# Two transformer layers on one core: the row-maximum steps of layer two's attention take other places among its projections

## The chip, the cores and the metric

The kernel runs on one core of one Trainium2 chip. Time is the device time of one execution in microseconds (us); before the change it is 1713.32 us, the median of three runs (1712.89 to 1716.47). The core's engines run beside each other, each through its own queue of instructions, in the order of that queue: TensorE (PE: matrix products and transposes, results in the accumulation memory PSUM), VectorE (DVE), ScalarE (ACT), GpSimd (POOL), and SyncE (SP), which issues most of the DMAs. An instruction starts when its queue has come to it and when what it waits for on other engines is done.

## The reference, cut to what matters

Two layers work on a sequence of 2048 tokens with 512 features. In each, a branch of attention and a feed-forward branch read the same normalised input, and both are added to the stream. Layer one is linear attention beside a mixture of 16 experts. Layer two, where the change lies, is

```
qkv  = xn @ w_qkv                          # xn: 2048 x 512, w_qkv: 512 x 1536
q, k = rope(rmsnorm(q)), rope(rmsnorm(k))  # per head; 16 heads of 32
s    = q @ k.T / sqrt(32), masked: 0 <= i - j <= 1024
out  = softmax(s) @ v @ w_out
idx  = top 256 tokens by xn . w_router     # these go through a small block of their own
```

The softmax needs the largest score of every row (query and head). This kernel computes the scores twice: once early, only to take the maxima, and once later, transposed, for the probabilities. The change moves pieces of the first of these two passes.

## The kernel before, in words

**Stages.** Layer one fills the span up to about 721 us. From there to 1014 us the loop `for t in range(NT)` (line 959) goes over 16 tiles of 128 tokens and projects each to q, k and v: the stage of the change. From 1014 to 1330 us the 256 chosen tokens pass their own attention and feed-forward block, and from 1330 us to the end come the probabilities and the output of layer two's attention.

**One token tile of the stage.** For `j` = 0, 1, 2 (q, k, v) PE makes four products of 128x128 by 128x512 into one PSUM tile `pj` (pool `ps4`, three buffers); the document calls them Q0..Q3, K0..K3, V0..V3. Each is two matmul records in the trace, at line 965. After q come the four transposes of the next tile's input (`turned`, tile `tr`), after k those of the *previous* tile's finished q, after v those of its k (`turned_qk`, line 776, tile `trqk`). All these transposes, and those of the maxima (`tn`), share one PSUM buffer, pool `ps_t4`; it comes free when ACT or DVE has copied its content out. At the end of a tile `normed_qk` (line 748) is issued: ACT squares q and k out of PSUM (line 754), DVE sums them per head (`rr`, line 755), ACT takes a root, DVE a reciprocal (line 79), two DVE multiplications (line 758) write `qk` and so free q's and k's `pj` buffers, and POOL (DVE for the last tile) applies the rotation (lines 763 to 773).

**The steps.** `maxima(i, ps_a)` (line 616) is a generator. Each of its steps, for one group of four heads and one chunk of keys, makes the scores of 128 queries on PE (line 633: four heads side by side, 32 rows each; eight records), adds masks where the chunk lies at an edge (lines 639, 641), and lets DVE reduce the 128x1024 to 128x2048 scores to maxima (line 645). A step issues no DMA. The scores lie in the tile `pa`, four PSUM banks, with **one** buffer: a step's products wait until the reduction of the step before has read it. After the last step of a query tile come four small reductions (lines 649 to 653), and with the step after that the transposes `tn` and a copy to `negT` on ACT. The 16 query tiles make 144 steps.

**Where steps are written.** `early = Steps(ps_a)` hands them out. `early.some(below)` (line 675) adds 0.9 to a balance and issues a step for each whole one, if one is allowed: query tiles lower than `below` alone, since a tile's q and k must have been transposed. A refused call sets the balance to zero. Before the change there are five calls a tile: after Q1, after q's product and the input transposes, after K1, after k's product and the transposes of q, and after v's product and the transposes of k. From the rate and the limits follow 65 steps: 62 in the loop from the end of tile 1 on, in the later tiles five and four in turn (five in the odd ones), and three written after the loop. The 79 that remain are spread over the next stage at (144 - done) / 182 per unit of work (line 1005).

**The routing.** `routing()` (line 783) finds the 256 tokens by counting: six scans of a 2048-wide row on DVE (line 853, `ge_h` and `ge_l`), each with small PE products (`pc_h`, `pc_l`) in the shared buffer and short work on DVE and POOL, after a row has gone out to DRAM and back by SP's queue; then lists are made on POOL. It is a generator too; `next(route)` is called after the second product of q, k and v, and after each whole product.

**What sets the order.** The loops give a *written* order. The queues do not follow it to the letter: a planner at build time lays the instructions out per engine by its own durations, and puts an instruction whose buffer or input it expects to be missing behind later ones that are ready. So PE's order in the trace is the written order with some steps put off by a few products.

Of the kernel before, what the change touches and what calls it, by code (L numbers as in the profile page):

```python
# [38 lines left out]
def two_layer_kernel(ctx: ExitStack, tc: tile.TileContext, a: dict, out: bass.AP):  # L39
# [29 lines left out]
    def load(eng, dst, src):  # L69
        eng.dma_start(out=dst, in_=src)  # L70
# [45 lines left out]
    def scopy(o, i):  # L116
        S.copy(o, i)  # L117
# [10 lines left out]
    with ExitStack() as l0:  # L128
# [208 lines left out]
        with ExitStack() as p3:  # L337
# [127 lines left out]
            for b in range(NTB):  # L465
# [39 lines left out]
                if b == NTB - 1:  # L505
# [15 lines left out]
                    def turned(t, pool, tag):  # L521

                        xn = xnq.pop(t)
                        if t + 2 < NT:
                            load_xn(t + 2)
                        xnt = xt4.tile([P, NC, P], F32, tag="xnt", name=f"xnt_{t}")
                        transpose4(
                            pool, lambda c: xn[:, c * P : (c + 1) * P], xnt, f"tr2_{t}", scopy, tag
                        )
                        return xnt  # L530
# [11 lines left out]
                for i in range(TB // P):  # L542
                    t = b * (TB // P) + i
                    xr.append(wk.tile([P, D], F32, tag="xr", name=f"xr_{t}", bufs=4))
                    load(nc.sync, xr[i], res_d[t * P : (t + 1) * P, :])
                for i in range(TB // P):
                    t = b * (TB // P) + i
# [172 lines left out]
    early = Steps(ps_a)  # L720


    with p4:
# [24 lines left out]
        def normed_qk(t, pp):  # L748

            qk = wk.tile([P, 2, HEADS, HD], F32, tag="qk", name=f"qk_{t}")  # L750
            t1 = wka.tile([P, 2, HEADS, HD], F32, tag="t1", name=f"t1_{t}")
            rr = wka.tile([P, 2, HEADS], F32, tag="rr", name=f"rr_{t}")
            for j in range(2):
                S.activation(t1[:, j].rearrange("p h d -> p (h d)"), pp[j], AF.Square)
            V.tensor_reduce(rr, t1, AX.X, ALU.add)
            rsqrt_into(rr, rr, eps_h)
            for j in range(2):
                V.tensor_tensor(  # L758
                    qk[:, j], pp[j].rearrange("p (h d) -> p h d", d=HD),
                    rr[:, j].unsqueeze(2).to_broadcast([P, HEADS, HD]), ALU.mult,  # L760
                )
            rope = V if t == NT - 1 else G
            rope.tensor_tensor(
                t1, qk, cosg[:, t].unsqueeze(2).to_broadcast([P, 2, HEADS, HD]), ALU.mult
            )
            t2 = wka.tile([P, 2, HEADS, HD], F32, tag="t2", name=f"t2_{t}")
            for lo, s0 in ((0, HH), (HH, 0)):
                rope.tensor_tensor(
                    t2[:, :, :, lo : lo + HH], qk[:, :, :, s0 : s0 + HH],
                    sing[:, t, :, lo : lo + HH].unsqueeze(2).to_broadcast([P, 2, HEADS, HH]),  # L770
                    ALU.mult,
                )
            rope.tensor_tensor(qk, t1, t2, ALU.add)
            return qk

        def turned_qk(t, qk, j):
            dst, cp = ((qT, scopy), (kT, vcopy))[j]
            transpose4(
                ps_t, lambda g: qk[:, j, 4 * g : 4 * g + 4, :].rearrange("p h d -> p (h d)"),
                dst[:, :, t * P : (t + 1) * P], f"trqk_{t}_{j}", cp,  # L780
            )
# [174 lines left out]
        route, gathering = routing(), []  # L956
        early.place(ps_t, "tr", 0.9)
        last_qk = None
        for t in range(NT):
            pp = []  # L960
            for j in range(3):
                pj = ps.tile([P, D], F32, tag="pj", name=f"p{j}_{t}")
                for c in range(NC):
                    w = w_v[:, c, :] if j == 2 else w_qk[:, c, j * D : (j + 1) * D]
                    PE.matmul(pj, xnt[:, c, :], w, start=c == 0, stop=c == NC - 1)  # L965
                    if c == 1:

                        if j < 2:
                            early.some(t - 1)
                        if t > 0:  # L970
                            next(route, None)
                pp.append(pj)
                if t > 0:
                    next(route, None)
                if j == 0 and t < NT - 1:
                    next_xnt = turned(t + 1, ps_t, "tr")
                    if t + 1 in (NT - 5, NT - 2, NT - 1):
                        gathering.append(t)
                elif j > 0 and last_qk is not None:
                    turned_qk(t - 1, last_qk, j - 1)  # L980
                early.some(t if j == 2 else t - 1)
            xnt = next_xnt
            vt = wk.tile([P, D], F32, tag="vt", name=f"vt_{t}")
            scopy(vt, pp[2])
            load(nc.sync, v_d[t * P : (t + 1) * P, :], vt)
            last_qk = normed_qk(t, pp)
# [517 lines left out]
```

## Time and profile before

| what | value |
|---|---|
| median of three runs | 1713.32 us |
| the profiled execution: its own time / its span | 1715.47 / 1713.8 us |
| PE busy over the span | 1657.4 us (97%) |
| DVE busy over the span | 982.5 us (57%) |
| stage of the change, 721 to 1014 us: PE busy / idle | 268.5 / 24.5 us |
| the same stage: DVE / ACT / POOL busy | 192.6 / 56.8 / 140.9 us |

In the rows of the profile, "busy" sums the time of instructions; "idle before" is the time that an engine waited ahead of a group, with the engine, tile and line that ended the wait. PE is the engine that is nearly always busy, so time is lost where PE waits. PE's weight loads stand as an engine of their own (PEld); they overlap the products, and a wait there is not by itself lost time. The sign `x6` behind a form counts records; two records are one product of 128x512. PEclk is the share of the full clock that PE was granted.

### The profile page before, as it was taken

The page shows a single profiled execution, that of the slowest core. Times are in us where ns is not written, and L with a number is a line of the kernel's source. Part 1 is how long each engine was busy: PE and PEld are TensorE (multiplying, and loading weights), DVE is VectorE, ACT ScalarE, POOL GpSimd, SP SyncE. Part 2 cuts the span into 40 slices and gives each one's busy share as a digit, 9 for nine tenths or more (in the row PEclk, how much of TensorE's full clock was granted, in tenths as well). Part 3 has the DMA queues.
Part 4 walks back from the last instruction along what each step waited for, and adds up shares of the span by engine and source line. Part 5 has one row for each costly group of instructions (what it writes and reads, how often), then busy time and mean ns, then how long its engine had stood idle before and what let it go on. Part 6 is the DMA issues. An engine that isn't in the chain of part 4 may idle for free.

```text
span 1713.8 us, 20410 instructions
## 1 busy us (share of the span) xinstructions
PE 1657.4 (97%) x8114; PEld 743.6 (43%) x8114; DVE 982.5 (57%) x1256; ACT 588.2 (34%) x939; POOL 500.0 (29%) x398
## 2 busy tenths in 40 slices
PE   8999999999999999989999989899999999999999
PEld 3445444444444444444443434454564333333343
DVE  4754746345445543357566676675555477557565
ACT  3213333243253344221111110431100566447473
POOL 3230000000000200053574423330000677558584
PEclk9999999999999999999999999999899999999999
DMA  9411001120030431111010034112232300110101
GB/s 360 169 37 47 25 25 37 47 88 25 25 111 25 94 104 50 62 56 56 25 32 26 28 118 153 62 50 74 74 99 74 99 1 2 50 50 2 50 1 38
DMA packets 62384, 109.23 MB, mean 64 GB/s; under 512 B 12528, under 2 KB 14064, under 8 KB 61520
## 3 DMA queue, kind: packets, MB, share of 16 engines
q1 hardware_dynamic: 55856, 106.12, 18.7%
q0 software_dynamic: 1152, 1.21, 0.4%
q10 hardware_dynamic: 5280, 0.59, 0.3%
q8 instruction: 63, 1.03, 0.3%
q14 instruction: 33, 0.27, 0.1%
HBM read 86.24 MB, written 21.67 MB: 63 GB/s over the span
## 4 chain that ended last, share of the span: by engine, by line
PE 81%; DVE 10%; ACT 2%; DMA 2%; POOL 2%; issue 2%; SPq 0%; DVEq 0%; POOLq 0%; ACTq 0%
PE ea L494 6%; PE acc L478 6%; PE eg L492 6%; PE ps L1296 6%; PE pa L633 6%; PE p L965 6%; PE av L1370 5%; PE po L553 3%; PE pq L367 3%; PE po L1340 3%; PE gx L242 3%; DVE mx L645 3%; PE mg L1210 2%; PE pao L1175 2%; PE pm L1225 2%; PE po L555 2%
## 5 line engine op out<-in xcount | busy, mean ns | idle before, releaser
L645 DVE TENSOR_REDUCE mx<-pa 128x4 f32<-128x1536 f32 (+3 forms) x144 | 252.9, 1756 | 151.2 <-PE pa L641 72.2
L1403 POOL TENSOR_TENSOR acc<-acc,pt 128x1024 f32<-128x1024 f32 (+2 forms) x110 | 252.9, 2328 | 96.6 <-DVE acc L1403 43.4
L1330 ACT ACTIVATE pt<-ps 128x1024 f32<-128x1024 f32 (+3 forms) x208 | 181.4, 924 | 108.1 <-PE ps L1319 61.5
L1403 DVE TENSOR_TENSOR acc<-acc,pt 128x1024 f32<-128x1024 f32 (+1 forms) x80 | 144.4, 1832 | 103.9 <-POOL acc L1403 103.9
L633 PE MATMUL pa<-kT,qT 32*128 32x384 f32 (+3 forms) x1152 | 139.8, 541 | 19.8 <-DVE mx L645 16.1
L350 ACT ACTIVATE r_e<-eg 128x512 f32<-128x512 f32 x128 | 75.9, 594 | 201.6 <-PE eg L492 194.4
L1296 PE MATMUL ps<-qT,kT 32*128 32x512 f32 (+3 forms) x1152 | 139.9, 524 | 0.0
L352 DVE TENSOR_TENSOR h<-ea,r_e 128x512 f32<-128x512 f32 x128 | 87.2, 685 | 84.5 <-ACT r_e L351 83.5
L743 POOL TENSOR_TENSOR cosg<-cosg,gam 128x512 f32<-128x512 f32 x2 | 2.5, 1264 | 442.7 <-DVE gam L740 442.7
L492 PE MATMUL eg<-xl,rwgT 128*128 128x512 f32 x256 | 130.7, 592 | 0.0
L494 PE MATMUL ea<-xw,rw1T 128*128 128x512 f32 x256 | 130.7, 592 | 0.0
L478 PE MATMUL acc<-h,rw2T 128*128 128x512 f32 x256 | 129.2, 592 | 0.0
L965 PE MATMUL p<-w_qk,xnt 128*128 128x512 f32 x256 | 123.2, 604 | 2.3 <-DVE qk L758 2.3
L1370 PE MATMUL av<-pt,v 128*32 128x512 f32 (+3 forms) x1024 | 100.8, 482 | 0.0
L1296 PEld LDWEIGHTS ps<-qT,kT 32*128 32x128 f32 x1152 | 54.7, 183 | 94.7 <-issue 65.8
L633 PEld LDWEIGHTS pa<-kT,qT 32*128 32x128 f32 x1152 | 46.8, 185 | 103.3 <-DVE mx L645 64.9
L488 DVE TENSOR_TENSOR xw<-xw,xl 128x512 f32<-128x512 f32 x64 | 43.8, 685 | 83.5 <-DMA xw<-w_d 83.2
L351 ACT ACTIVATE r_e<-r_e 128x512 f32<-128x512 f32 x128 | 80.3, 629 | 5.7 <-ACT r_e L350 1.9
L478 PEld LDWEIGHTS acc<-h,rw2T 128*128 128x128 f32 x256 | 48.6, 190 | 61.3 <-issue 52.1
L492 PEld LDWEIGHTS eg<-xl,rwgT 128*128 128x128 f32 x256 | 48.6, 190 | 61.2 <-issue 61.0
L494 PEld LDWEIGHTS ea<-xw,rw1T 128*128 128x128 f32 x256 | 48.6, 190 | 61.2 <-issue 59.3
L288 PE MATMUL pk<-k_wT,xnT 128*128 128x512 f32 x128 | 61.3, 622 | 3.5 <-ACT xnT L117 3.5
(336 smaller groups left out, 2420.0 us busy)
## 6 DMA issues: line engine op xcount, KB each, us to landing
xw<-w_d SPq DMA_DIRECT2D x64, 256.0 KB, 3.2
x<-in_x SPq DMA_DIRECT2D x16, 256.0 KB, 4.7
res_d<-x SPq DMA_DIRECT2D x16, 256.0 KB, 2.1
xr<-res_d SPq DMA_DIRECT2D x16, 256.0 KB, 4.2
xn_d<-xn SPq DMA_DIRECT2D x16, 256.0 KB, 3.0
res_d<-xr SPq DMA_DIRECT2D x16, 256.0 KB, 3.1
xnq<-xn_d SPq DMA_DIRECT2D x16, 256.0 KB, 2.8
v_d<-vt SPq DMA_DIRECT2D x16, 256.0 KB, 2.0
```

What stands on the lines that cost most here:

```text
L351: S.activation(r, r, AF.Square)
L352: V.tensor_tensor(dst, pa, r, ALU.mult)
L478: PE.matmul(acc, rw2T[:, j, e, :], h, start=e == 0 and j == 0, stop=e == E - 1 and j == 1,)
L492: PE.matmul(pg, rwgT[:, e, hb], xl, start=True, stop=True)
L494: PE.matmul(pa, rw1T[:, e, hb], xw, start=True, stop=True)
L633: PE.matmul(pS[:, h, : w * P], qT[r, g, i * P : (i + 1) * P], kT[r, g, ks], start=True, stop=not (edge or last),)
L645: V.tensor_reduce(mx[:, g, :, c], pS[:, :, : w * P], AX.X, ALU.max)
L965: PE.matmul(pj, xnt[:, c, :], w, start=c == 0, stop=c == NC - 1)
L1296: PE.matmul(pS[h // 2][:, h % 2, t0 * P - q0 : (t1 + 1) * P - q0], kT[r, g, kb * P : (kb + 1) * P], qT[r, g, t0 * P : (t1 + 1) * P], start ...
L1330: S.activation(pT[:, :, :n], pS[hp][:, :, :n], AF.Exp)
L1370: PE.matmul(self.av[h * HD : (h + 1) * HD, t0 * P - o : (t1 + 1) * P - o], vs[kb // 4][:, kb % 4, hs], got[h // 2][:, h % 2, t0 * P - q0 : ...
L1403: eng.tensor_tensor(part, part, got[hp][:, :, : q1 - q0], ALU.add)
```

## The change

In a tile, q and k each had a call of `early.some` after the second product and one at the end (for q behind the transposes of the next input, for k behind those of the previous q). Now both have one after the first product and one after the third. v keeps its call behind the transposes of k. The routing's calls stay where they were. As the number, the order and the limits of the calls are the same, the same 65 steps are issued by the same calls in turn; only their written places differ.

```
                     PE.matmul(pj, xnt[:, c, :], w, start=c == 0, stop=c == NC - 1)
-                    if c == 1:
-
-                        if j < 2:
-                            early.some(t - 1)
-                        if t > 0:
-                            next(route, None)
+
+                    if c % 2 == 0 and j < 2:
+                        early.some(t - 1)
+                    if c == 1 and t > 0:
+                        next(route, None)
                 pp.append(pj)
                 if t > 0:
                     next(route, None)
                 if j == 0 and t < NT - 1:
                     next_xnt = turned(t + 1, ps_t, "tr")
                     ...
                 elif j > 0 and last_qk is not None:
                     turned_qk(t - 1, last_qk, j - 1)
-                early.some(t if j == 2 else t - 1)
+                if j == 2:
+                    early.some(t)
```

The written order of a tile, with S for a call, T for transposes of the next input, tq and tk for those of the previous tile's q and k:

```
before:  Q0 Q1 S  Q2 Q3 T  S  K0 K1 S  K2 K3 tq S  V0 V1 V2 V3 tk S
after:   Q0 S  Q1 Q2 S  Q3 T  K0 S  K1 K2 S  K3 tq V0 V1 V2 V3 tk S
```

## The prediction

> **What bounds the kernel now.** I read the page first, then the stage of the change in stretches, then who waits for whom in it, then PE's order in time.
>
> The page says that PE is the engine that counts:
>
> ```profile
> PE 1657.4 (97%) x8114; PEld 743.6 (43%) x8114; DVE 982.5 (57%) x1256; ACT 588.2 (34%) x939; POOL 500.0 (29%) x398
> ```
>
> The change keeps every PE instruction, so it can only move PE's idle time. Four stretches of the stage, from the first step on (length, then busy time of PE, PEld, DVE, ACT, POOL, then clock):
>
> ```profile
> 747.00:843.00 96.00, 86.08 (x450) 39.93 (x449) 65.39 (x89) 17.64 (x34) 43.80 (x55) 0.98 0.12 38
> 843.00:917.00 74.00, 70.04 (x341) 30.64 (x340) 47.71 (x47) 13.76 (x28) 50.56 (x48) 1.00 0.14 29
> 917.00:990.00 73.00, 69.10 (x339) 29.38 (x338) 49.91 (x47) 13.51 (x26) 31.59 (x24) 1.00 0.09 27
> 990.00:1014.00 24.00, 19.59 (x106) 8.55 (x108) 17.82 (x21) 5.07 (x11) 6.18 (x4) 1.00 0.07 23
> ```
>
> PE's idle time is 9.9, 4.0, 3.9 and 4.4 us, 22.2 us in all: 1.3% of the kernel, and the most that any order could save. The waits of the stage (time in all, times, longest) name the steps' one buffer:
>
> ```profile
> PEld pa L633 <- DVE mx L645: 36.0, 34, 2.9
> ...
> PE pa L633 <- DVE mx L645: 11.3, 9, 2.1
> ```
>
> Half of the idle time, 11.3 us, is a step that waits for the reduction before it. What a reduction costs on DVE, by width, with the sum that stands beside it in the queue:
>
> ```profile
> L645 DVE TENSOR_REDUCE mx<-pa 128x4 f32<-128x1536 f32 x34 | 59.7, 1755 | 32.1 <-PE pa L641 14.6 <-PE pa L633 12.7 <-PE pa L639 4.9
> L645 DVE TENSOR_REDUCE mx<-pa 128x4 f32<-128x2048 f32 x16 | 36.6, 2290 | 16.7 <-PE pa L641 11.0 <-PE pa L633 5.7
> ...
> L755 DVE TENSOR_REDUCE rr<-t 128x32 f32<-128x1024 f32 x16 | 19.5, 1216 | 14.6 <-ACT t L754 14.5
> ```
>
> Now PE in order of time, through tile 14 (start, length, instruction, count; an idle time stands at the end):
>
> ```profile
> 973.12 2.84 PE L965 MATMUL p<-w_qk,xnt 128*128 128x512 f32 x6
> 975.89 0.93 PE L633 MATMUL pa<-kT,qT 32*128 32x384 f32 x8
> ...
> 977.90 0.60 PE L110 MATMUL tr<-ident,xnq 128*128 128x128 f32 x4
> 978.33 1.02 PE L965 MATMUL p<-w_qk,xnt 128*128 128x512 f32 x2
> 979.29 0.93 PE L633 MATMUL pa<-kT,qT 32*128 32x384 f32 x8
> ...
> 980.38 2.79 PE L965 MATMUL p<-w_qk,xnt 128*128 128x512 f32 x6
> 983.11 0.93 PE L633 MATMUL pa<-kT,qT 32*128 32x384 f32 x8
> ...
> 984.46 2.74 PE L965 MATMUL p<-w_v,xnt 128*128 128x512 f32 x6
> 988.32 0.93 PE L633 MATMUL pa<-kT,qT 32*128 32x384 f32 x8 [1.12 <-DVE mx L645]
> ```
>
> The four steps of this tile are written after Q1, T, K1 and tq. They run after Q2, K0, K3 and V2: one, one, two and three products later. So the place in the code is only the earliest place; the planner holds a step until it expects `pa` free. In tiles 8 to 15 I count 36 steps: 28 run later than written, 8 where they are written, and three of those 8 are the ones behind tk, which the change leaves alone. Between two steps PE nearly always has three products, or two and a set of transposes: 2.6 or 2.2 us, at 0.86 us a product (980.38 to 983.11 holds three and some 0.1 us of changeover) and 0.43 us a set (977.90 to 978.33). A reduction of 1.76 or 2.29 us and its start need that much.
>
> **The change part by part.**
>
> *The four moved calls.* They come earlier by one product (after Q1 to Q0, K1 to K0) or by one product and four transposes (T to Q2, tq to K2): 0.86 and 1.29 us. Two of the new gaps hold two products, 1.72 us, less than the trace shows between steps. A step held by `pa` stays where it is whatever is written: 28 of 36 cost and gain nothing, and their cover is that same reduction. What can move is a tile whose first step runs as written, tiles 9, 11 and 15: there the first step goes up by one product, and those behind it may follow.
>
> *Tile 9.* Its third step closes a query tile and brings `tn` with it, in the one buffer that tq needs next:
>
> ```profile
> 889.78 0.40 PE L658 MATMUL tn<-ident_b,parts 128*128 128x128 bf16 x4
> 890.01 1.08 PE L965 MATMUL p<-w_qk,xnt 128*128 128x512 f32 x2
> 891.77 0.66 PE L110 MATMUL trqk<-ident,qk 128*128 128x128 f32 x4 [0.68 <-ACT t L754]
> ```
>
> One product earlier, two products (1.72 us) lie between `tn` and tq, ACT copies `negT` (0.59 us a copy) before it has K3 to square, and the 0.68 us go: **-0.7 us**. Its bounds are 0 and -0.90 us, the whole gap from 890.87 (890.01 and one product) to 891.77. *Tile 11* has no idle time to give between 917 and 935 us: 0.
>
> *Tile 15.* The last tile is closed by DVE, whose queue is full from 1000.76 us to the end of the stage: sum of squares, roots, two steps' reductions and the rotation. The step of 1000.02 us goes one product up, to 999.16; its reduction can start 1.29 us after that (as at 992.58 and 993.87), at 1000.45 in place of behind the sums, so the run starts 0.31 us earlier with the same work: **-0.3 us**. Bounds: -1.79 us, the wait ahead of the step at 1005.23, which then has its buffer in time; and +1.22 us, if the sum is pushed back by its own length and the rotation ends later.
>
> *Tiles 2 to 7*, with the routing. A step's reduction now stands before the routing's piece at the end of q and of k, where it stood behind it; a scan there is 2.34 us of DVE. The trace does not show that order. The end of gain is the idle time of the stretch, -9.9 us. The end of loss is the five scans of 2.34 us between 747 and 843 us, each in front of one more step that now runs free: +11.7 us. I take 0, by the nearest row, the same steps in tiles 8 to 15, where 28 of 36 do not move and the rest gain 1.0 us.
>
> *Queues passed.* ACT: `negT` of a query tile comes before instead of behind other copies, counted in tile 9. POOL and SP: steps put nothing on them, and the routing's order on them stays. Beyond the stage the 79 other steps keep their rate, as 65 are done either way: 0, within what the profile's own executions differ by.
>
> *The clock.* In the stretch that ends the routing's scans PE's clock was halved once, after a wait of 2.2 us for the routing's `base_l`:
>
> ```profile
> 810.00:825.00 15.00, 12.82 (x58) 5.31 (x59) 10.32 (x11) 2.04 (x4) 6.82 (x4) 0.89 0.05 18
> ```
>
> An 11% loss over 15 us is 1.65 us. A wait moved there or away is worth that once more: ±1.65 us in the range, 0 in the sum. The Trainium skill ("TensorE: Matmul & The Clock Gate", Part 1: The HAM clock gate) says the clock drops after an idle window of about 3.4 us; by that rule no wait here would reach it and the term would be nil. The row shows a drop after 2.2 us, and the row decides.
>
> Another page of the Trainium skill ("Trainium Kernel Development and Optimization", Best Practices) says that regular gaps can mean that PSUM has run out. Read against this change: with one `pa` buffer no new place helps, and the sum by that rule would be 0 instead of -1.0 us.
>
> **Sum**: -0.7 - 0.3 + 0 = -1.0 us. The profiled execution took 1715.47 us (span 1713.8 and 1.67 around it), 2.15 us over the median of the runs, and would become 1714.5. On the median, 1713.32 - 1.0 = **1712.3 us**.
>
> **The rivals.**
>
> *A: a reduction gets ahead of the row sums, slower.* The fourth step is now written before K3, so its reduction can stand in DVE's queue before `rr` of the same tile. Then the squares, root and products wait, and q's and k's `pj` buffers, which the next tile's Q0 needs, come free later. For it: in tile 11 this already happens (a reduction of 2.29 us starts at 927.84, `rr` at 930.05), and the buffers come free at 933.39 for a Q0 at 934.13, a margin of 0.74 us. Against it: in tiles 9 and 10 the margin is 3.1 and 2.8 us. It decides once a reduction beyond those of now costs over 0.74 us there. Price: 2.29 - 0.74 = 1.55 us a tile, and 2.29 for a step that then waits too; over the six odd tiles from 5 to 15 9.3 to 13.7 us if it strikes each, about half of it if it strikes half: +5.5 us, 1718.8 us.
>
> *B: the waits of the scan stretch go, faster.* There steps are short of DVE because scans cut in. If steps come earlier than the scans, half of the 9.9 us idle and one halved clock of 1.65 us go: -1.0 - 5.0 - 1.65 = -7.6, 1705.7 us. For it: the waits at 768, 788 and 820 us (2.7, 2.1 and 2.2 us) are all in this stretch. Against it: an earlier reduction only trades places with a scan on the same engine.
>
> *C: nothing happens.* If the planner holds the free steps too, PE's order is the same: 1713.3 us. Against it: eight steps do run where they are written.
>
> **How the numbers follow.** About 0.2% (3.4 us) is what a measurement of this kernel can tell from no change. Chances: the forecast 0.44, C 0.07, A 0.27, B 0.22. Forecast and C lie within 0.2%; 0.04 of the forecast's share falls outside, half on each side, by the scan stretch; 0.01 each of A and B falls inside, where they strike one tile alone. So: faster 0.23, same 0.49, slower 0.28. The likeliest case alone has 1709 to 1716 (tile 15's bounds, the clock's 1.65 us, and a scan of 2.34 us either way). The range of 8 in 10 goes out to where B and A have struck for the most part: 1706.5 to 1719.5.
>
> **What would show it.** Right: steps of even tiles where they are now, those of tile 9 one product up, the 0.68 us before tq gone; PE's idle time from 843 to 990 us at about 7.2 us, now 7.9; the waits of `pa` for `mx` near 11 us. Wrong: idle time that PE spends on `qk` (line 758) at the head of a tile means A; a first stretch with 5 us of idle time means B; steps that all follow their written places would mean that the buffer isn't what holds them.

## The result and the profile after

The kernel after the change takes 1718.29 us (median of 13 executions, 1714.86 to 1721.27), the kernel before 1713.35 us beside it (13 executions, 1711.33 to 1717.48): a ratio of 1.0026 (the recorded one, which is not the quotient of the two medians), with a 95% interval of 1.0018 to 1.0035. That is 4.5 us more (3.1 to 6.0), where the prediction said 1.0 us less. The profiled execution of after took 1718.57 us (span 1716.9).

The page's line of busy times, after:

```profile
PE 1662.0 (97%) x8114; PEld 746.0 (43%) x8114; DVE 982.8 (57%) x1256; ACT 588.3 (34%) x939; POOL 499.5 (29%) x398
```

PE has the same 8114 records and is busy 4.6 us longer, while its idle time over the span fell from 56.4 to 54.9 us: the same work went at a lower clock. In the profiled executions 17.1 us of the span passed at half clock before and 34.1 after. The four stretches that the prediction read, after (length, busy time of PE, PEld, DVE, ACT, POOL, then the granted clock), and a fifth, shorter one, here with its row of before behind it:

```profile
747.00:843.00 96.00, 87.63 (x461) 40.72 (x460) 65.87 (x89) 18.33 (x35) 43.48 (x56) 0.98 0.12 39
843.00:917.00 74.00, 67.26 (x321) 29.44 (x320) 46.85 (x45) 13.79 (x27) 49.57 (x47) 0.98 0.14 26
917.00:990.00 73.00, 68.27 (x335) 29.01 (x335) 49.18 (x46) 12.91 (x25) 30.72 (x24) 1.00 0.08 27
990.00:1014.00 24.00, 19.91 (x102) 8.70 (x100) 18.05 (x20) 5.45 (x11) 6.13 (x4) 0.96 0.07 23
886.00:893.00 7.00, 3.69 (x18) 2.02 (x18) 3.21 (x6) 1.40 (x3) 3.19 (x2) 0.76 0.00 0
```

```profile
886.00:893.00 7.00, 6.32 (x29) 2.48 (x26) 5.66 (x7) 1.72 (x3) 5.63 (x4) 1.00 0.57 40
```

PE's idle time from 843 to 990 us is 11.5 us; it was 7.9, and the prediction said 7.2. Most of what came on lies in the 7 us of the last two rows: PE is busy there for 3.7 us, where it was 6.3, and its clock is 0.76. PE's waits from 721 to 1024 us, after:

```profile
PE pa L633 <- DVE mx L645: 11.5, 9, 1.8
PE trqk L110 <- POOL qk L773: 5.3, 3, 3.3
...
PE trqk L110 <- DVE qk L773: 2.2, 1, 2.2
PE trqk L110 <- DVE base_l L860: 1.3, 1, 1.3
...
PE p L965 <- DVE qk L758: 1.0, 1, 1.0
```

and two of them before:

```profile
PE pa L633 <- DVE mx L645: 12.3, 10, 2.1
...
PE trqk L110 <- POOL qk L773: 0.3, 1, 0.3
```

The waits for the steps' one buffer are nearly what they were. New are 5.3 us in which PE waits for POOL's rotation, and 2.2 us for the last tile's rotation on DVE. PE in order of time around tile 9, after:

```profile
882.76 1.14 PE L633 MATMUL pa<-kT,qT 32*128 32x512 f32 x8
883.84 0.40 PE L658 MATMUL tn<-ident_b,parts 128*128 128x128 bf16 x4
884.07 1.94 PE L965 MATMUL p<-w_qk,xnt 128*128 128x512 f32 x4
889.32 1.05 PE L110 MATMUL trqk<-ident,qk 128*128 128x128 f32 x4 [3.31 <-POOL qk L773]
890.30 1.66 PE L633 MATMUL pa<-kT,qT 32*128 32x384 f32 x8
```

`tn` has gone up by one product and two products lie between it and tq, as forecast. But PE now stands 3.31 us for POOL, and behind that the step's records take 1.66 us where they took 0.93: the clock is halved. POOL's own timeline shows why it is late, after:

```profile
869.33 1.03 POOL L922 DMA_INDIRECT list_d<-tokc,place  x1 [0.16 <-POOL qk L773]
...
876.58 0.19 POOL L920 CAST place<-pos 128x4 int32<-128x4 f32 x1 [2.43 <-DMA list_d<-tokc,place]
...
881.05 0.96 POOL L922 DMA_INDIRECT list_d<-tokc,place  x1 [0.30 <-issue]
882.03 2.37 POOL L763 TENSOR_TENSOR t<-qk,cosg 128x1024 f32<-128x1024 f32 x1
```

DVE had written tile 8's `qk` by 872.4 us. POOL comes to it at 882.0, because eight of the routing's scatters (line 922) stand ahead of it in POOL's queue, and between the two fours of them POOL waits 2.43 us for their transfers. The start and the end of the same rotation in before:

```profile
884.46 2.37 POOL L763 TENSOR_TENSOR t<-qk,cosg 128x1024 f32<-128x1024 f32 x1
...
889.37 2.34 POOL L773 TENSOR_TENSOR qk<-t,t 128x1024 f32<-128x1024 f32 x1
```

It ends at 891.71 us, and PE starts tq at 891.77. So POOL had no time to spare in before either; the idle time of 0.68 us ahead of tq, which the row put down to ACT, ended with POOL's rotation too.

Adding up tiles (from PE's first product of q to the next tile's; the last from there to the first product of `v2p`):

| tiles | before | after | what the two traces differ in |
|---|---|---|---|
| 0 to 4 | 81.5 | 80.9 | |
| 5 to 7 | 59.7 | 56.1 | the wait of 2.17 us for `base_l` at 820 us and the half clock behind it are gone |
| 8 and 9 | 36.1 | 40.8 | waits for POOL of 1.64 and 3.31 us, half clock at 889 us |
| 10 and 14 | 36.2 | 36.2 | |
| 11 to 13 | 56.0 | 56.9 | one step more in 11, one less in 13 |
| 15 and what follows | 51.5 | 54.1 | wait of 2.22 us for DVE at 1011.67, 10.24 us of half clock behind it |

The gain of 3.6 us in tiles 5 to 7 is given back, and 1 us more, in tiles 8 and 9. From tile 5 on the rows add up to +4.5 us: -3.6, +4.7, 0, +0.8 and +2.6. Outside the stage the order is the same, and yet the half clock behind the second norm, at 1206.8 us in both, lasts 13.65 us after and 10.24 before.

### The profile page after: what moved, and what is told of

Read it like the earlier page. It is cut to its first block, busy times and chain, and to the rows that moved or that the text cites. A ratio compares the mean times of both kernels' runs of the same rounds, so it can differ in the third digit from the quotient of the medians.

```text
span 1716.9 us, 20410 instructions
## 1 busy us (share of the span) xinstructions
PE 1662.0 (97%) x8114; PEld 746.0 (43%) x8114; DVE 982.8 (57%) x1256; ACT 588.3 (34%) x939; POOL 499.5 (29%) x398
## 4 chain that ended last, share of the span: by engine, by line
PE 81%; DVE 10%; POOL 3%; DMA 2%; ACT 2%; issue 2%; SPq 0%; DVEq 0%; POOLq 0%; ACTq 0%
PE ea L494 6%; PE eg L492 6%; PE acc L478 6%; PE ps L1296 6%; PE pa L633 6%; PE av L1370 5%; PE p L965 5%; PE po L553 3%; PE pq L367 3%; PE po L1340 3%; PE gx L242 3%; DVE mx L645 2%; PE mg L1210 2%; PE pao L1175 2%; PE pm L1225 2%
## 5 line engine op out<-in xcount | busy, mean ns | idle before, releaser
L633 PE MATMUL pa<-kT,qT 32*128 32x384 f32 (+3 forms) x1152 | 141.9, 550 | 18.6 <-DVE mx L645 14.5
```

Of the source, the lines that this page charges most:

```text
L633: PE.matmul(pS[:, h, : w * P], qT[r, g, i * P : (i + 1) * P], kT[r, g, ks], start=True, stop=not (edge or last),)
```

## The experiments

All times are medians; "before" in a sentence is the kernel before on the same chip. A difference in us is the ratio's, on 1713.4 us; in brackets is a 95% interval. The recorded ratio is not the quotient of the medians: with new places up to tile 8 and the scatters spaced, for one, it says -4.5 us where the medians are 3.2 us apart.

**Parts of the change, by tile.** The two edited conditions take a test of the tile; where it fails, a tile has the places of before. For all tiles but the last:

```
-                    if c % 2 == 0 and j < 2:
+                    if (c % 2 == 0 if t < NT - 1 else c == 1) and j < 2:
                     ...
-                if j == 2:
-                    early.some(t)
+                if j == 2 or not (t < NT - 1):
+                    early.some(t if j == 2 else t - 1)
```

> New places in tiles 2 to 14, old places in the last tile. Theory T (tail: the loss lies behind the last tile, where the profile after has a wait of 2.2 us for the rotated q and then a halved clock of 10.2 us): 2.5 us less than the changed kernel, about 1715.8 us, and the clock is whole from 1012 to 1023 us. Theory P (POOL: the loss lies in tile 9, where PE waits 3.3 us for POOL's rotation of tile 8): at most 0.5 us less than the changed kernel, 1717.8 to 1718.3 us. Rival A of the prediction (the fourth step's reduction ahead of the row sums, in every odd tile): one tile in six, about 0.8 us less.

Measured: 1718.22 us, ratio 1.0024 (1.0013 to 1.0034). The last tile's stretch went back to 51.8 us and no half clock followed, in one trace; the median did not move.

With `t != 9` as the test:

> New places in all tiles but tile 9, which has the old ones. Theory P: POOL's queue is what tile 9 waits for, whatever its order on PE; the wait ahead of the transposes of tile 8's q stays at 3 us or more, the time at 1718 us (within 0.5 us of the changed kernel). Rival A: the order of tile 9 makes the loss, so the wait there falls to the 0.7 us of before and the time by 2.6 us to 1715.7 us. Theory T: no difference from the changed kernel.

Measured: 1719.05 us, 1.0031 (1.0019 to 1.0044). The wait for POOL did not go with the place: PE waits 1.96 us in tile 8 and 1.59 in tile 9.

With `t <= 8`:

> New places up to tile 8, old places from tile 9 on. Theory P: PE comes to tile 9 some 4 us earlier than in the kernel before (counted from the start of the stage) and waits there 3 us or more for POOL; from tile 10 on it runs as before: 1713.3 to 1714.3 us. Theory T: the tail is as before too, so 1713.3 us less the early tiles' gain of up to 4 us, if the wait in tile 9 is absent: 1709 to 1713 us. Rival A: the odd tiles from 9 on are as before, 3, 5 and 7 keep their loss: half of 5 us, 1715.8 us.

Measured: 1719.17 us, 1.0035 (1.0022 to 1.0047). Waits for POOL of 2.04 and 1.64 us, though tile 9 has its old places. So it is not tile 9's step that brings the waits for POOL, and what is left is that PE is early.

With `t >= 9`:

> Old places up to tile 8, new places from tile 9 on. Theory P: no early gain, so no wait for POOL over 1 us in tile 9. Theory T: the tail's 2.5 us remain: 1715.8 us, and the halved clock after 1012 us is there. Rival A: four of the six odd tiles keep the loss: 3.3 us, 1716.6 us, with idle time of PE on the row multiplications at the head of tiles 10, 12, 14.

Measured: 1717.99 us, 1.0026 (1.0014 to 1.0038), and PE waits for POOL for no more than the 0.3 us of before. None of the four undid the loss, so neither the last tile's places nor tile 9's are all of it. And the new places from tile 9 on cost as much by themselves as the whole change, +4.5 us, with POOL in time: the waits for POOL cannot be all of it either.

What differed between executions was the granted clock, which every execution reports. Over 296 executions (16 kernels, and before in five calls; the three kernels with the first fills, below, are left out), with each kernel's own mean taken out, the time falls by 1.35 us for each 0.001 of granted clock (correlation -0.84). The mean clock was 0.9942 for before (129 executions) and 0.9913 for after (13): by that slope 3.9 of the 4.5 us would go with the clock. But the slope was found within kernels, and it is not shown to hold from one kernel to another: after with the scatters spaced (below) has a mean clock of 0.9912, as low as after's, and no loss, and new places in all tiles but the last have 0.9930 and 4.1 us of loss. Where most of the 0.003 comes from can be read: in the traces of all five kernels that have new places in the last tile and no products in its wait, 10.24 us of half clock stand at 1011 to 1018 us, which is 0.0030 of the span's clock; in the traces with old places there it is 3.41 us at most.

**Filling PE's waits.** Products that nobody reads were put where PE waits: behind the first chunk of queries and around the second norm of the gathered rows, in both orders, and in after also ahead of the last tile's closing step.

```
+        def fill(n, name):
+            pd = ps.tile([P, D], F32, tag="mm", name=f"fill_{name}")
+            for _ in range(n):
+                PE.matmul(pd, qT[:, 0, 0:P], kT[:, 0, 0:D], start=True, stop=True)
...
             if waiting is not None:
                 next(waiting)
+            else:
+                fill(7, "q2")
             turn()
...
+                if name == "b":
+                    fill((6, 4)[j], f"b{j}")
                 tp = ps.tile([P, NC, P], F32, tag="mm", name=f"trh_{name}_{j}")
...
         hT = rms_norm_T(xs, 1, "b")
+        fill(5, "b2")
```

> The order of before, with products that nobody reads put on PE at two places where it waits in both kernels: seven behind the first chunk of queries (a wait of 3.6 us, 1077 us) and fifteen in three groups around the second norm of the gathered rows (1206 us). Theory C (the loss is granted clock: each wait that the gate sees halves the clock for a multiple of 3.4 us): before loses 3.41 us and 10.24 us of half clock there in its profile, so that up to 6.8 us come back: 1707 to 1711 us, granted clock 0.997 to 0.998. Rival O (order: PE's waits cost what they last, and the clock is a passenger): the products fill idle time, 1713.4 us, at most 1 us more, whatever the clock shows.

Measured: 1720.78 us, 1.0028 (1.0018 to 1.0037), at a mean clock of 0.9981.

After with the same, and with three products in the tail:

```
+        pd = ps.tile([P, D], F32, tag="pj", name="pd")
+        for c in range(3):
+            PE.matmul(pd, xnt[:, c, :], w_v[:, c, :], start=True, stop=True)
         early.one(NT - 1)
```

> The order of after with the same 22 products and three more ahead of the last tile's closing step (the wait of 2.2 us at 1011.7 us, behind which the clock was halved for 10.24 us). Theory C: 3.41, 13.65 and 10.24 us of half clock go, up to 13.6 us come back: 1705 to 1711 us, and the difference to the kernel before with the same fills is under 2 us. Rival O: 1718 us, and 4.7 us over before with the fills.

Measured: 1728.98 us, 1.0067 (1.0052 to 1.0082).

The three products in the tail alone:

> After with the three products in the tail alone; the closing step may then come ahead of the last transposes. Theory C: the 10.24 us of half clock go, -5.1 us at most: about 1713.5 us. Theory T (only the tail's own 2.5 us count): 1715.8 us. Rival O: 1718.3 us or 1.3 us more.

Measured: 1722.5 us, 1.0036 (1.0021 to 1.0051). All three fills were mis-sized: a product takes two records, 0.86 us, and I had counted 0.43, so they outlasted the waits. The first two runs were repeated with four, three, two and two products, and two in the tail; the tail alone was not.

> The first fills were too long: a product of 128x512 takes two passes, 0.86 us and not 0.43, so PE stood 8 us longer at the three places, against some 3.3 us that the clock gave back. Here the order of before with four products in the wait of 3.6 us at 1077 us (3.44 us) and three, two and two in the waits around the second norm (2.6, 1.7 and 1.7 us). Theory C: the 3.41 and 10.24 us of half clock go and nothing is pushed back, up to -6.8 us: 1707 to 1710 us, granted clock about 0.998. Rival O: PE's work of these stretches ends with another engine's chain anyway, so the clock there is worth nothing: 1713 to 1715 us at a clock of 0.998.

Measured: 1709.59 us, 0.9981 (0.9972 to 0.9990): 3.3 us faster than before, at a clock of 0.9985. The two stretches in before:

```profile
1070.00:1085.00 15.00, 11.57 (x64) 7.05 (x63) 7.81 (x10) 4.83 (x14) 6.44 (x10) 0.89 0.27 88
1200.00:1220.00 20.00, 17.15 (x72) 9.69 (x69) 10.02 (x13) 6.34 (x11) 0.00 (x0) 0.74 0.18 53
```

and in before with the fills:

```profile
1070.00:1085.00 15.00, 14.49 (x84) 7.64 (x77) 10.37 (x13) 7.73 (x25) 4.15 (x6) 1.00 0.25 89
1200.00:1220.00 20.00, 19.83 (x101) 11.71 (x101) 10.36 (x13) 5.55 (x11) 0.00 (x0) 1.00 0.14 52
```

More records in the same time, and the clock is whole. So lost clock is lost time here: theory C's first half holds, if at half the size forecast (-3.3 of "up to -6.8").

> The order of after with the same eleven products and two in the tail's wait of 2.2 us. Theory C: up to 13.6 us of lost clock come back, less what drops elsewhere: 1707 to 1712 us, within 2 us of before with the same fills. Rival O: 4 to 5 us over before with the fills, 1718 us.

Measured: 1717.78 us, 1.0026 (1.0015 to 1.0036), clock 0.9956. The clock rose, and after stayed 8.2 us behind before with the fills. From the first product of `v2p` to the end the two traces take the same 668.1 us (before 671.6), so the 8.2 us lie ahead of it, in the stage. Theory C's second half falls: the halved clock behind the stage is not what the change cost. Tiles 9 and 10 of this trace take 24.2 and 20.2 us (before 18.7 and 18.6), with 3.5 us of waiting for POOL in tile 9 and half clock in each of them.

**POOL's queue.** One number of the routing: how many pieces of the stage lie between two fours of scatters.

```
                         in_=tokc[:, 4 * n + i, :], in_offset=None,
                     )
-                for _ in range(4):
+                for _ in range(8):
                     yield
```

> After with eight pieces of the stage between two scatters of the routing where there were four, so that POOL does not stand behind their transfers when the rotation of tile 8 comes. Theory P (the wait of 3.3 us in tile 9 is what the change cost): -3.3 us and 1.7 us of half clock behind it, 1713.3 us. Theory C: the wait goes, but the granted clock stays near 0.991 unless the drop at 889 us goes with it: 1714 to 1717 us.

Measured: 1715.97 us, 1.0001 (0.9991 to 1.0011). The change's loss is gone, with every place of a step as in after. In the trace PE's waits for POOL fall from 5.3 to 2.4 us: the one in tile 9 is gone, the one in tile 8 is left:

```profile
876.88 0.66 PE L110 MATMUL trqk<-ident,qk 128*128 128x128 f32 x4 [2.05 <-POOL qk L773]
```

Combined with the second fills:

> After with the scatters eight pieces apart and the same fills. Theory C: its time at whole clock is the lowest seen (1701 us by time and granted clock of eleven runs), so with the three drops filled 1705 to 1709 us. Rival O: 1716 us, as with the scatters alone.

Measured: 1709.99 us, 0.9988 (0.9979 to 0.9997), and 7.8 us under the same kernel with the scatters close. POOL's timeline there:

```profile
871.96 2.35 POOL L763 TENSOR_TENSOR t<-qk,cosg 128x1024 f32<-128x1024 f32 x1 [2.95 <-DVE qk L758]
874.27 2.51 POOL L768 TENSOR_TENSOR t<-qk,sing 128x512 f32<-128x512 f32 x2
876.86 2.34 POOL L773 TENSOR_TENSOR qk<-t,t 128x1024 f32<-128x1024 f32 x1
879.14 0.19 POOL L920 CAST place<-pos 128x4 int32<-128x4 f32 x1
```

POOL waits for tile 8's `qk`, and not `qk` for POOL; the rotation starts at 871.96 us, 10 us earlier than in after, and the scatters come behind it. Tile 9 takes 18.0 us there, and 24.2 us in the run with the close scatters. The same spacing in the order of before:

> The order of before with the scatters eight pieces apart. If spacing them only undoes what the change brought (POOL late in tile 9), 1713.5 to 1715.5 us as before; if POOL's queue is late in any order, 2 to 3 us less, 1711 to 1712 us.

Measured: 1713.01 us, 1.0000 (0.9991 to 1.0009). In the old order the spacing is worth nothing, to within 1.5 us, so it is the new order that made POOL's queue a bound.

The spacing with new places up to tile 8 alone, which had cost most:

> New places up to tile 8, old ones from tile 9, scatters eight pieces apart. Theory P (the steps of tiles 6 and 7 gain 3 to 4 us, and POOL's late rotation gives it back in tiles 8 and 9): from the tile lengths of before and of the spaced runs, tiles 5 to 10 take 111.1 in place of 114.4 us, so 3.3 us under before, about 1710 us. If the new places cost in themselves: 1715 to 1719 us, as without the spacing.

Measured: 1711.59 us against 1714.76, 0.9974 (0.9963 to 0.9985): 4.5 us faster than before, where the same places with the scatters close were 6.0 us slower. The stretch of 886 to 893 us, in which after had 3.69 us of PE and a clock of 0.76:

```profile
886.00:893.00 7.00, 7.00 (x38) 3.23 (x34) 6.21 (x6) 2.27 (x5) 1.26 (x2) 1.00 0.00 0
```

With the fills added:

> The same with four, three, two and two products in PE's waits behind the stage. Theory P and C added: 3.3 us under before with the fills, 1706 to 1707 us. If spacing and fills only put the change right: 1709 to 1710 us.

Measured: 1711.13 us against 1714.76, 0.9963 (0.9946 to 0.9980), -6.3 us by the ratio and -3.6 by the medians. Both are faster than before; what the fills add to the spacing here is within the intervals.

The opposite, two pieces between scatters in the order of before (`range(2)`):

> The order of before with two pieces of the stage between two scatters where there were four: POOL stands behind more transfers at once. Theory P: waits of PE for POOL's rotation appear around tiles 7 to 9 and cost 2 to 5 us, 1715 to 1718 us, with no place of a step changed. If the places are the cost: 1713.4 us.

Measured: 1717.86 us against 1714.76, 1.0014 (1.0003 to 1.0024). +2.4 us: slower as forecast, but by another way than forecast. DVE in that trace, and PE behind it:

```profile
858.94 1.22 DVE L755 TENSOR_REDUCE rr<-t 128x32 f32<-128x1024 f32 x1 [2.14 <-DMA list_d<-tokc,place]
```

```profile
860.81 0.61 PE L658 MATMUL tn<-ident_b,parts 128*128 128x128 bf16 x4 [2.43 <-DVE parts L653]
```

`place`, from which the scatters read their addresses, takes its buffers from the same tag as `rr`; the row sums wait until the scatters have read it, and the maxima's last reductions stand behind the sums on DVE. The routing's scatters hold up the stage by two ways, POOL's queue and this buffer.

**The tiles from 9 on.** New places in the last tile alone (`t == NT - 1`):

> Old places, and new ones in the last tile alone. By the stretches from the last tile's first product to the first product of v2p (51.5 us before, 54.0 to 54.2 with the new places) and the half clock of 10.24 us behind its wait: +2.5 to +4 us, 1716 to 1717.5 us. By the step of my prediction for that tile: -0.3 us.

Measured: 1714.6 us against 1714.76, 0.9997 (0.9985 to 1.0008). The trace shows what I feared:

```profile
1010.29 0.63 PE L110 MATMUL trqk<-ident,qk 128*128 128x128 f32 x4 [2.22 <-DVE qk L773]
```

and 10.24 us of half clock behind it (0.63 over 1008 to 1022 us), 2.8 us more up to `v2p`. The median shows no loss; between -2.6 and +1.4 us it can't say more, so the 2.8 us of the trace are not shown as time.

In tiles 9 to 14 alone (`8 < t < NT - 1`):

> New places in tiles 9 to 14 alone. If these tiles cost what the run with new places from tile 9 on measured: +4 us, 1717.5 us. If the tile lengths of the profiles are all (0.6 to 0.9 us more in tiles 11 to 13): +0.9 us, 1714.3 us, and the rest of the 4.5 us came from the last tile's wait and its half clock together with these.

Measured: 1716.05 us against 1713.86, 1.0014 (1.0003 to 1.0025), +2.4 us: between the two expectations. In its trace tiles 11 to 13 take 0.8 us more and 1.7 more for a half clock behind this wait, which before has too, at full clock:

```profile
966.91 0.93 PE L633 MATMUL pa<-kT,qT 32*128 32x384 f32 x8 [1.79 <-DVE mx L645]
```

In all tiles but the last, with the scatters spaced:

> New places in all tiles but the last, scatters eight pieces apart. If tiles 9 to 14 cost 4 us: level with before, 1713.4 us, as with new places everywhere. If they cost 0.9 us: 3.6 us under before (1709.8 us), and the last tile is what separates it from the spaced run with new places everywhere.

Measured: 1712.38 us against 1713.86, 0.9993 (0.9983 to 1.0003), -1.2 us.

With spaced scatters the parts can be put in a row, each against before: no new places 0.0, up to tile 8 -4.5, up to tile 14 -1.2, in all +0.2 us. Each of the four has an interval of about ±1.8 us, a difference of two some ±2.5. So the first part is a gain, tiles 9 to 15 together cost 4.6 us, as much as the new places from tile 9 on with the scatters close; of that tiles 9 to 14 have 3.3, and the last tile's 1.4 is not told from nothing. With the scatters close the first part is +6.0 us and all of it +4.5.

## Why the prediction was wrong

**The step that failed** is "POOL and SP: steps put nothing on them, and the routing's order on them stays", costed at nothing. Both statements are true, and the conclusion that it costs nothing was not: PE came to tile 8's transposes about 5 us earlier than before, POOL's rotation only 2.4 us earlier, since the scatters in its queue are paced by their own transfers. The term measured 4.3 us (after against after with spaced scatters, 1.0026 to 1.0001, each within some ±1.7 us), and 7.8 us with the fills. It is not the whole error: the terms of tiles 9 to 15, -1.0 us in the sum, measured +4.5 us alone and +4.6 with the scatters spaced, and the 0 of tiles 2 to 7 was a gain of 4.5. Taken in this order the measured +4.5 us is made up of -4.5, +4.6 and, from the scatters, +4.3, each with its interval; with the scatters close the tiles up to 8 alone measured +6.0, so the parts do not add up in every order. I had listed the queues that steps are moved past, but not asked who is late when PE is early; the end of the rotation, 0.06 us ahead of PE's start, was in the trace of before.

**The clock**, "±1.65 us in the range, 0 in the sum". The row that it was built on, a drop after 2.2 us, was right, and the page's idle window was rightly set aside. But the prediction began with "it can only move PE's idle time", and in the profiled executions PE's idle time fell by 1.5 us while its busy time rose by 4.6. I priced one wait moved there or away, and the runs show the mean clock 0.003 lower, most of it in the 10.24 us of half clock behind the last tile's new wait of 2.22 us. What that costs in time stays open: the last tile's places cost -0.5 us alone and 1.4 us with the scatters spaced, neither told from nothing. Without the wait for POOL in tile 9 the mean clock was no higher, 0.9912 with spaced scatters; with the fills it was, 0.9987 with the scatters spaced and 0.9956 without.

**Tile 9, -0.7 us.** The order came as forecast, one product up. The term rested on a row that I misread: the 0.68 us were not ACT's alone. ACT's instruction named there ended at 891.73 us and POOL's rotation at 891.71; in the run with new places in the last tile alone, which has before's order here, the wait at the same place is put down to POOL:

```profile
890.35 0.65 PE L110 MATMUL trqk<-ident,qk 128*128 128x128 f32 x4 [0.43 <-POOL qk L773]
```

What was earlier on PE had to wait longer for it: 3.31 us. The bounds, 0 and -0.90, had no upper side.

**Tiles 2 to 7, 0.** In the trace they gain: tiles 5 to 7 take 3.6 us less, because a step leaves tile 6 for tile 5, the wait for `base_l` falls away and its half clock with it. The nearest row, tiles 8 to 15, was the wrong one, and rival B's mechanism was at work in one of its three waits. The runs with spaced scatters show it as time (-4.5 us); in after it is given back in tiles 8 and 9.

**Tile 11, 0, and tile 15, -0.3.** Tiles 11 to 13 take 0.8 us more in every trace with their new places. In tile 15 the wait of 1.79 us did go, which was the far end of its bounds; the transposes then waited 2.22 us for DVE's rotation, the other end. The last tile's stretch is 2.6 us longer for it in the traces; alone, the time of it stays unresolved between -2.6 and +1.4 us.

**The prediction's rivals.** A had the right sign by a mechanism that didn't come: idle time on `qk` of line 758 fell from 2.3 to 1.0 us. C falls, as PE's order changed. **What held**: the buffer of the steps is the bound of the stage (waits of 11.5 us, forecast near 11). That steps of even tiles stay held in tiles 8, 10 and 14; in tile 12 it did not: with a step more in tile 11 the order is another one up to tile 13.

**Open.** The tile lengths add up to the whole change and, within the intervals, to new places up to tile 8 and up to tile 14 with the scatters spaced; they do not to new places in the last tile alone, nor up to tile 8 with the scatters close. Why the latter measured 6.0 us slower, when their trace shows 3.7 us of waiting for POOL in tiles 8 and 9 and is the fastest execution of that kernel; the interval (3.8 to 8.1) and the spread of the clock leave room, but the sum is not shown. And whether the 2.4 us of tiles 9 to 14 are more than 0.8 us of order with the clock's chance on top.

## What to carry to other kernels

When a change makes the bounding engine early, list the other queues that feed it and how late each may be: a gain ends at the first queue that keeps its pace, and that queue can be nowhere near the edit. A wait on PE can cost more than its length once it is long enough to take the clock, so a wait of 2 us that appears is priced with a halved clock behind it; filling such waits with idle products was worth 3.3 us in the order of before, and cost 4.8 where the products were longer than the waits. A slope of time against clock, found among the executions of one kernel, is not a price for the clock that another kernel has. Before blaming a place, test the thing that made somebody late: here one number in the routing turned +4.5 us into 0, and with a part of the change into -4.5 us.

## What the runs showed of the hardware

PE's clock is halved in pieces of 3.41 us (3.41, 6.83, 10.24 and 13.65 us), and the pieces lie on a fixed grid: in after they start at 766.6, 889.4, 1012.3, 1080.6 and 1206.9 us, whose distances are 36, 36, 20 and 37 times 3.413 us. Against the start of the span the grid lies elsewhere in every trace (1.88 us into its piece in before, 1.96 in after, 3.06 in before with the second fills). The Trainium skill ("TensorE: Matmul & The Clock Gate", Part 1: The HAM clock gate) says that the window of 3413 ns is free-running; the traces agree. It speaks of an idle window, and here the traces differ: I laid each of 17 traces (all but those of the first fills) on its own grid and took the share of a window in which PE had a product running (ends as the profile models them). Over 100 to 1690 us, at full clock, windows with less than 40% were followed by half clock in 34 of 34 cases, with 40 to 50% in 24 of 53, with 50 to 70% in 10 of 192, and above 70% in none of some 7500. So two microseconds of waiting inside one window are enough, and the same wait split by a window's edge is not: the wait of 1.79 us near 967 us stands in all twenty traces and halved the clock in one. Executions of one kernel differ by up to 12 us (1711.9 to 1724.0 in the run with new places up to tile 8, at clocks of 0.996 and 0.989); a grid that isn't tied to the span's start would do that, though no run here set it.
